# A deformable attention's depthwise taps: products on ScalarE and row sums on VectorE in place of multiply-adds on VectorE, small ScalarE work dealt out in smaller portions, three loads issued later

## The chip, the cores and the metric

The kernel runs on one core of a Trainium2 chip. The metric is device time in microseconds, the median of three runs: 3592.72 us before the change (3592.03 to 3593.57). A profiled execution, from which all views below come, had a span of 3587.1 us and a mean granted TensorE clock of 0.995.

## The reference, cut to what matters

Four layers follow one another on an image of 2 x 512 x 32 x 32. The change lies in the first, a deformable attention with 8 groups of 64 channels. Only this part matters here:

```python
q = _gconv1x1(xn, qw)                                  # per group: 64 channels, 32 x 32
qg = q.reshape(b * GROUPS, DH, H, W)
off = conv_general_dilated(qg, off_dw_w, (4, 4), ((1, 1), (1, 1)),
                           feature_group_count=DH)     # 6 x 6 taps, stride 4: 8 x 8 out
off = gelu(off + off_dw_b, approximate=False)
off = tanh(einsum('bchw,oc->bohw', off, off_pw_w)) * OFF_SCALE
...                                                    # the 64 sampling points, k and v from them
bias = sign(pos) * log1p(abs(pos))                     # 1024 pixels x 64 points x 2
bias = relu(bias @ cpb_w1 + cpb_b1)                    # to 128
bias = relu(bias @ cpb_w2 + cpb_b2)                    # 128 to 128
bias = (bias @ cpb_w3 + cpb_b3)                        # to 1
attn = softmax(einsum('bhid,bhjd->bhij', qh, kh) + bias)
out = einsum('bhij,bhjd->bhid', attn, vh)
```

The bias network runs for every pixel and every sampling point of every group. It is by far the most work of the layer; the taps, the sampling and the softmax are small beside it.

## The kernel before

Two groups make a pair; there are eight pairs `t` (two images, four each), and one loop of 256 steps (32 for each pair) runs through the bias network of all of them. A step handles four rows of points. `first` adds the two scaled tables on VectorE (line 487), into a ring of twelve buffers; `second` multiplies by `cpb_w2` on TensorE (line 504, into one of three PSUM tiles with the tag "z") and ScalarE evicts with Relu (line 512); `joined` adds two evicted parts on VectorE (line 517); a GpSimd transfer accumulates two of those; `third` (line 527) contracts with the last weights.

```python
for i in range(steps + 2):
    ...
    if i % 4 == 0 and i // 4 + 1 in tabs_of:
        scale_tabs(i // 4 + 1)
    for k, part in enumerate((1, 0, 3, 2)):
        p = 4 * i + AHEAD + k
        if p < 4 * steps:
            h1s[p] = first(p)
        if i < steps:
            parts.setdefault(i, {})[part] = second([h1s[4 * i + point] for point in range(4)], part)
        if k == 1 and i - 1 in parts:
            other = joined(parts.pop(i - 1), 2)
            if i < steps:
                nc.gpsimd.dma_start(out=joins[i - 1], in_=other, accum_op=ALU.add)
            ...
        if k % 2:
            next(behind, None)                 # one portion of the small work
        if k == 3 and i < steps:
            joins[i] = joined(parts[i], 0)
    ...
    if i >= 5 and i % 4 == 1:
        t, r = divmod(i - 5, NR)
        ...
        third(sim, r, [joins.pop(i - 5 + j) for j in range(4)])
        if r == NR - 4:
            assert next(behind, None) is None
            scores(t, sim)
            behind = chain(finish(t, sim),
                           offsets(t + 2) if t + 2 < NT else iter(()),
                           samples(t + 1) if t + 1 < NT else iter(()))
```

All that belongs to a pair beside the bias network is in generators, from which the loop takes one portion (up to the next `yield`) after every second of the four parts of a step, so two per step. Instructions of an engine keep the order of the program. `offsets` has the taps:

```python
def offsets(t):
    qpad = one.tile([P, 36, 36], F32, name="qpad", tag="pixels")
    ...                                        # q on TensorE, into qpad by ScalarE; two yields
    qv = qpad.rearrange("p (a i) (c k) -> p a i c k", i=4, k=4)
    acc = one.tile([P, HD, WD], F32, name="acc")
    for tap in range(36):
        ky, kx = divmod(tap, 6)
        src = qv[:, ky // 4 : ky // 4 + HD, ky % 4, kx // 4 : kx // 4 + WD, kx % 4]
        w = col("dw_w", tap)
        if tap == 0:
            nc.vector.tensor_scalar(acc, src, w, None, ALU.mult)              # line 331
        else:
            nc.vector.scalar_tensor_tensor(acc, src, w, acc, ALU.mult, ALU.add)  # line 333
        if tap == 33:
            table(AF.Gelu)
        if tap % 3 != 1:
            yield
    accf = acc.rearrange("p y x -> p (y x)")
    act = actbd[t % 2]
    for h in range(2):
        r = slice(h * DH, (h + 1) * DH)
        nc.scalar.activation(act[r, r], accf[r], AF.Gelu, bias=col("dw_b")[r])   # line 342
    yield
    ...                                        # tanh, positions, their logarithms, out to memory
```

`table` is a small activation that brings the function's table onto ScalarE ahead of its use. The softmax of a pair is in `finish`, the tables of the loop in `load_tabs` and `scale_tabs`:

```python
for g in range(16):                            # line 564
    nc.scalar.activation(atv[:, g, :], ptv[:, g, :], AF.Exp, bias=mx[:, g : g + 1],
                         accum_out=sm[:, g : g + 1])
    if g % 4 == 3:
        yield
nc.vector.reciprocal(sm, sm)

def scale_tabs(c):                             # two tables of 128 x 512 for every fourth step
    tx, ty = tabs_of[c]
    if c == 0:
        ...                                    # the same on VectorE
    else:
        nc.scalar.activation(tx, tx, AF.Identity, bias=col("cpb_b1"), scale=col("cpb_w1", 0))  # 473
        nc.scalar.mul(ty, ty, col("cpb_w1", 1))                                                # 474
```

Ahead of the loop, weights of a later layer are folded on TensorE (`fold`), and the order of the loads there is:

```python
def late_loads():
    load_groups("vw")
    nc.sync.dma_start(out=xs[1], in_=...)      # the second image
    nc.sync.dma_start(out=ow, in_=...)         # output weights
...
load_tabs(0)
scale_tabs(0)
late_loads()
for _ in range(3):
    advance(small_steps)
    advance(fold_steps)
drain(fold_steps)
...
for p in range(AHEAD):
    h1s[p] = first(p)                          # first(0) issues load_tabs(1)
```

Of the kernel before, what the change touches and what calls it, by code (L numbers as in the profile page):

```python
# [11 lines left out]
F32 = mybir.dt.float32  # L12
AF = mybir.ActivationFunctionType
# [66 lines left out]
def kernel(ctx: ExitStack, tc: tile.TileContext, a: dict, out: bass.AP):  # L80
# [56 lines left out]
    def layer0(l0, fold_d, t2_b, o2_b):  # L137
# [166 lines left out]
        def table(function):  # L304
            nc.scalar.activation(trial[:, 1:2], trial[:, 0:1], function)
# [4 lines left out]
        def offsets(t):  # L310
            b, pr = divmod(t, NPAIR)
            qpad = one.tile([P, 36, 36], F32, name="qpad", tag="pixels")
            nc.gpsimd.memset(qpad, 0.0)
            pq = zt([P, HW], "pq")
            for half in range(2):
                n = slice(half * HALF, (half + 1) * HALF)
                nc.tensor.matmul(pq[:, n], qws[:, pr, :], xs[b][:, pr, n], start=True, stop=True)
            yield
            nc.scalar.activation(
                qpad[:, 1:33, 1:33], pq.rearrange("p (y x) -> p y x", x=W), AF.Identity, bias=qb[:, pr : pr + 1]  # L320
            )
            yield

            qv = qpad.rearrange("p (a i) (c k) -> p a i c k", i=4, k=4)
            acc = one.tile([P, HD, WD], F32, name="acc")
            for tap in range(36):
                ky, kx = divmod(tap, 6)
                src = qv[:, ky // 4 : ky // 4 + HD, ky % 4, kx // 4 : kx // 4 + WD, kx % 4]
                w = col("dw_w", tap)
                if tap == 0:  # L330
                    nc.vector.tensor_scalar(acc, src, w, None, ALU.mult)
                else:
                    nc.vector.scalar_tensor_tensor(acc, src, w, acc, ALU.mult, ALU.add)
                if tap == 33:
                    table(AF.Gelu)
                if tap % 3 != 1:
                    yield
            accf = acc.rearrange("p y x -> p (y x)")
            act = actbd[t % 2]
            for h in range(2):  # L340
                r = slice(h * DH, (h + 1) * DH)
                nc.scalar.activation(act[r, r], accf[r], AF.Gelu, bias=col("dw_b")[r])
            yield
            po = zt([P, 2], "po")
            nc.tensor.matmul(po, act, col("pw_w", 0, 2), start=True, stop=True)
            th = two.tile([P, 2], F32, name="th")
            nc.scalar.activation(th, po, AF.Tanh)
            yield

            nxy = two.tile([P, 2], F32, name="nxy")  # L350
            nc.vector.scalar_tensor_tensor(nxy, th, 4.0, cs("gxy"), ALU.mult, ALU.add)
            nc.vector.tensor_scalar(nxy, nxy, 2.0 / 7.0, -1.0, ALU.mult, ALU.add)

            pos = two.tile([P, 2, 32], F32, name="pos")
            nc.vector.tensor_tensor(
                pos,
                cs("gq").unsqueeze(1).to_broadcast([P, 2, 32]),
                nxy.unsqueeze(2).to_broadcast([P, 2, 32]),
                ALU.subtract,
            )  # L360
            gp = two.tile([P, 2], F32, name="gp")
            nc.vector.tensor_scalar(gp, nxy, 1.0, W / 2.0, ALU.add, ALU.mult)
            nc.vector.tensor_scalar(gp, gp, -0.5, None, ALU.add)
            gps[t] = gp
            table(AF.Ln)
            yield
            sgn = two.tile([P, 2, 32], F32, name="sgn")
            nc.scalar.activation(sgn, pos, AF.Sign)
            nc.scalar.activation(pos, pos, AF.Abs)
            nc.scalar.activation(pos, pos, AF.Ln, bias=1.0)  # L370
            yield
            nc.vector.tensor_mul(pos, pos, sgn)
            nc.sync.dma_start(out=slog_d[t].rearrange("x p i -> p x i"), in_=pos)
            tables.add(t)
# [12 lines left out]
        def samples(t):  # L387
# [23 lines left out]
            wx = one.tile([P, P], F32, name="wx")  # L411
            nc.scalar.activation(wx, gpb[:, 0, :], AF.Abs, bias=cs("px"))
            nc.scalar.activation(wx, wx, AF.Relu, bias=1.0, scale=-1.0)
            wy = one.tile([P, 8, P], F32, name="wy")
            for k in range(8):
                nc.scalar.activation(wy[:, k, :], gpb[:, 1, :], AF.Abs, bias=cs("py", k))
                if k % 3 == 1:
# [46 lines left out]
                nc.sync.dma_start(out=tab, in_=src[:, rc * RCH : (rc + 1) * RCH, :].partition_broadcast(P))  # L464
                tabs_of[c].append(tab)

        def scale_tabs(c):
            tx, ty = tabs_of[c]
            if c == 0:
                nc.vector.tensor_scalar(tx, tx, col("cpb_w1", 0), col("cpb_b1"), ALU.mult, ALU.add)  # L470
                nc.vector.tensor_scalar(ty, ty, col("cpb_w1", 1), None, ALU.mult)
            else:
                nc.scalar.activation(tx, tx, AF.Identity, bias=col("cpb_b1"), scale=col("cpb_w1", 0))
                nc.scalar.mul(ty, ty, col("cpb_w1", 1))

        def first(p):

# [65 lines left out]
        def finish(t, sim):  # L543

            b, pr = divmod(t, NPAIR)
            if pr == 0:
                oTs[b] = one.tile([P, NPAIR, HW], F32, name="oT")
            oT = oTs[b]
            simb = two.tile([P, HW], F32, name="simb", tag="simb")
            nc.scalar.activation(simb, sim, AF.Identity, bias=simbias[t])  # L550
            yield
            table(AF.Exp)
            pt = zt([P, 8, P], "pt")
            for i in range(8):
                nc.tensor.transpose(pt[:, i, :], simb[:, i * P : (i + 1) * P], ident)
            ptv = pt.rearrange("p i (g j) -> p (i g) j", j=NJ)
            mx = two.tile([P, 16], F32, name="mx")
            nc.vector.tensor_reduce(mx, ptv, AX.X, ALU.max, negate=True)
            yield
            at = two.tile([P, 8, P], F32, name="at", tag="simb")  # L560
            atv = at.rearrange("p i (g j) -> p (i g) j", j=NJ)
            sm = two.tile([P, 16], F32, name="sm")
            for g in range(16):
                nc.scalar.activation(
                    atv[:, g, :], ptv[:, g, :], AF.Exp, bias=mx[:, g : g + 1], accum_out=sm[:, g : g + 1]
                )
                if g % 4 == 3:
                    yield
            nc.vector.reciprocal(sm, sm)
            nc.vector.tensor_tensor(atv, atv, sm.unsqueeze(2).to_broadcast([P, 16, NJ]), ALU.mult)  # L570
            yield
            last = t == NT - 1
            pps = []
            if last:

                pps = [zt([P, HW], "pp") for _ in range(2)]
                for m in range(2):
                    project_out(pps[m], m, range(NPAIR - 1 - m), oT)
            pa = zt([P, 8, P], "pa")
            for i in range(8):  # L580
                nc.tensor.transpose(pa[:, i, :], at[:, i, :], ident)
            if last:
                project_out(pps[1], 1, [NPAIR - 2], oT)
            aT = two.tile([P, HW], F32, name="aT", tag="simb")
            nc.scalar.copy(aT, pa.rearrange("p i j -> p (i j)"))
            yield
            pv = (ps_s if last else ps_z).tile([P, HW], F32, name="pv", tag="sim" if last else "z")
            for half in range(2):
                n = slice(half * HALF, (half + 1) * HALF)
                nc.tensor.matmul(pv[:, n], vbd[t], aT[:, n], start=True, stop=True)  # L590
                if last:
                    nc.scalar.copy(oT[:, pr, n], pv[:, n])
            if not last:
                nc.scalar.copy(oT[:, pr, :], pv)
            yield
            if pr < NPAIR - 1:
                return
            for m in range(CC):
                if m < len(pps):
                    pp = pps[m]  # L600
                    project_out(pp, m, [NPAIR - 1], oT)
                else:
                    pp = zt([P, HW], "pp")
                    project_out(pp, m, range(NPAIR), oT)
                nc.vector.scalar_tensor_tensor(xs[b][:, m, :], pp, col("out_b", m), xs[b][:, m, :], ALU.add, ALU.add)
                yield
# [103 lines left out]
        drain(steps)  # L710
        advance(small_steps, 2)
        load_tabs(0)
        scale_tabs(0)
        late_loads()
        for _ in range(3):
            advance(small_steps)
            advance(fold_steps)
# [11 lines left out]

        for p in range(AHEAD):  # L730
            h1s[p] = first(p)
        for i in range(steps + 2):
            if i == steps:
                (w1s,) = load_w(wa, "wa", [a["mlp_w1"]])
            if i % 4 == 0 and i // 4 + 1 in tabs_of:
                scale_tabs(i // 4 + 1)
            for k, part in enumerate((1, 0, 3, 2)):
                p = 4 * i + AHEAD + k
                if p < 4 * steps:
                    h1s[p] = first(p)  # L740
# [886 lines left out]
```

## Time and profile before

| what | value |
|---|---|
| median of three runs | 3592.72 us |
| loop of the first layer, from the first z to the last projection | 56.45 to 2138.5 us |
| one pair of the loop, from 836.28 to 1088.55 us | 252.27 us |
| in it: TensorE, VectorE, ScalarE busy | 249.18, 237.45, 170.21 us |
| z eviction on ScalarE (line 512, 128x1024) | 1.115 us, x1024 |
| sum of the tables on VectorE (line 487, 128x1024) | 1.22 us, x1024 |
| join on VectorE (line 517, 128x1024) | 1.28 us, x512 |
| scaling of a chunk's tables on ScalarE (lines 473 and 474) | 0.81 and 0.71 us, x63 each |

The profile gives, for one execution, the busy time of each engine, groups of instructions with their mean duration and the idle time ahead of them, a list of who waited for whom, and the chain of work that ended last: followed back from the last instruction, at each step to what released it or to the instruction before it on its engine. In the chain a line is start, duration, engine, tile and line of the program; "issue" is time in which nothing in the profile was waited for. A busy TensorE is not TensorE at its peak: a matmul of the z kind lasts 595 ns from start to end, but several run at once, so its pace has to be read from stretches of the chain. Idle time of an engine costs nothing where another one sets the pace.

### The profile page before, as it was taken

What the parts mean: (1) busy time and instruction counts of PE and PEld (TensorE: products, weight loads), DVE (VectorE), ACT (ScalarE), POOL (GpSimd) and SP (SyncE); (2) the same over time, 40 slices, a digit from 0 to 9 for tenths busy, and PEclk for the clock granted to TensorE, in tenths of its full rate; (3) what the DMA queues carried; (4) which work ended last, traced back from release to release, by engine and by line L of the source; (5) the groups of instructions that cost most, each with busy time, mean ns of one, the idle gap of its engine ahead of it and who ended that gap; (6) DMA issues with size and microseconds to landing.
All of it is one profiled execution on the core that took longest, in us unless ns stands there. A gap on an engine that the chain in (4) does not pass through costs nothing.

```text
span 3587.1 us, 57945 instructions
## 1 busy us (share of the span) xinstructions
PE 3529.7 (98%) x24777; PEld 1468.8 (41%) x24777; DVE 2507.3 (70%) x2930; ACT 1691.6 (47%) x2226; POOL 278.7 (8%) x326
## 2 busy tenths in 40 slices
PE   8999999999999999999999989999999999999999
PEld 4333333333333333233233339999633333444443
DVE  6999998998996998999998944554256365130223
ACT  3666666666664676667666631211244133111111
POOL 0111111111110111111111100000001000000000
PEclk9999999999999999999999999999999999999999
DMA  5454444454452444444444440000200000000000
GB/s 163 84 99 84 82 94 85 83 95 79 83 95 58 83 95 83 93 85 77 95 83 89 85 120 11 10 13 13 80 1 1 1 1 1 15 0 0 6 30 25
DMA packets 135963, 213.44 MB, mean 60 GB/s; under 512 B 14993, under 2 KB 93201, under 8 KB 134929
## 3 DMA queue, kind: packets, MB, share of 16 engines
q0 software_dynamic: 36720, 133.71, 19.8%
q1 hardware_dynamic: 98832, 75.41, 8.5%
q8 instruction: 197, 3.23, 0.4%
q14 instruction: 70, 0.57, 0.0%
q10 hardware_dynamic: 144, 0.52, 0.0%
HBM read 64.12 MB, written 10.75 MB: 21 GB/s over the span
## 4 chain that ended last, share of the span: by engine, by line
PE 80%; DVE 16%; issue 2%; ACT 2%; DMA 1%; SPq 0%; POOL 0%; POOLq 0%; DVEq 0%; ACTq 0%
PE z L504 33%; PE pw L135 6%; DVE wa L487 5%; PE pm L1226 5%; PE pma L135 5%; PE pmv L135 5%; DVE h L517 5%; PE pmb L135 4%; PE score L1337 4%; PE score L135 3%; PE pv L1385 3%; DVE h L487 3%; PE sim L527 2%; PE ppr L1257 2%; PE pmp L135 2%
## 5 line engine op out<-in xcount | busy, mean ns | idle before, releaser
L512 ACT ACTIVATE h<-z,b2h 128x1024 f32<-128x1024 f32 x1024 | 1134.5, 1115 | 662.9 <-PE z L504 635.8
L504 PE MATMUL z<-wa,cpb_w 128*32 128x512 f32 x10880 | 1202.0, 595 | 13.0 <-ACT h L512 13.0
L487 DVE CUSTOM_DVE_ANT_1 wa<-tab,tab 128x1024 f32<-128x1024 f32 x680 | 800.3, 1219 | 13.5 <-PE z L504 13.5
L504 PEld LDWEIGHTS z<-wa,cpb_w 128*32 128x32 f32 x10880 | 349.4, 110 | 824.5 <-issue 733.3
L517 DVE SCALAR_TENSOR_TENSOR h<-h,turn,h 128x1024 f32<-128x1024 f32 x512 | 655.0, 1279 | 21.9 <-ACT h L512 21.7
L504 PE MATMUL z<-h,cpb_w 128*32 128x512 f32 x5504 | 616.1, 597 | 14.2 <-ACT h L512 14.2
L487 DVE CUSTOM_DVE_ANT_1 h<-tab,tab 128x1024 f32<-128x1024 f32 x344 | 405.0, 1220 | 11.0 <-PE z L504 10.9
L746 POOL DMA_DIRECT2D h<-h x255 | 220.1, 863 | 1831.8 <-DVE h L517 806.3
L504 PEld LDWEIGHTS z<-h,cpb_w 128*32 128x32 f32 x5504 | 177.0, 110 | 426.9 <-issue 376.1
L1338 ACT ACTIVATE p<-score 128x1024 f32<-128x1024 f32 x144 | 139.5, 1021 | 184.8 <-PE score L1337 184.8
L135 PE MATMUL pw<-p,vT 128*128 128x512 f32 x512 | 221.8, 593 | 1.3 <-DVE y L1443 1.3
L1268 DVE TENSOR_TENSOR acc<-acc,p 128x2048 f32<-128x2048 f32 x56 | 128.8, 2301 | 105.1 <-ACT p L1338 57.8
L1121 ACT COPY p<-pma 128x128 f32<-128x128 f32 x70 | 18.6, 266 | 304.0 <-PE pma L135 304.0
L1270 DVE TENSOR_TENSOR acc<-p 128x2048 f32<-128x2048 f32 x12 | 27.5, 2291 | 183.6 <-ACT p L1472 110.0
L135 PEld LDWEIGHTS pw<-p,vT 128*128 128x128 f32 x512 | 97.0, 190 | 122.6 <-issue 121.0
L1113 DVE TENSOR_TENSOR upper<-pma,p 128x256 f32<-128x256 f32 x70 | 29.6, 423 | 163.4 <-ACT p L1121 163.3
L527 PE MATMUL sim<-h,w 128*32 128x512 f32 x1024 | 125.7, 599 | 6.6 <-DMA h<-h 6.6
L1337 PE MATMUL score<-q,k 64*128 64x512 f32 x512 | 127.2, 615 | 0.0
L1226 PE MATMUL pm<-hc,wa 128*64 128x512 f32 x512 | 122.4, 603 | 0.0
L1385 PE MATMUL pv<-p,vT 128*64 128x512 f32 x512 | 121.4, 595 | 0.0
L135 PE MATMUL score<-t,hc 128*128 128x512 f32 x256 | 110.2, 592 | 0.0
L1443 DVE TENSOR_TENSOR y<-pw,r 128x512 f32<-128x512 f32 x32 | 21.8, 682 | 115.8 <-PE pw L135 115.8
(299 smaller groups left out, 3057.8 us busy)
## 6 DMA issues: line engine op xcount, KB each, us to landing
h<-h POOLq DMA_DIRECT2D x255, 512.0 KB, 4.9
tab<-slog_d SPq DMA_DIRECT2D x128, 256.0 KB, 6.8
wa<-in_qkv_w SPq DMA_DIRECT2D x8, 768.0 KB, 6.3
xt<-in_xt SPq DMA_DIRECT2D x8, 512.0 KB, 4.9
wa<-in_mlp_w SPq DMA_DIRECT2D x4, 1024.0 KB, 10.1
wb<-in_mlp_w SPq DMA_DIRECT2D x16, 256.0 KB, 5.4
x_d<-x SPq DMA_DIRECT2D x32, 128.0 KB, 1.8
out<-x SPq DMA_DIRECT2D x16, 256.0 KB, 2.0
```

The costliest lines, as they stand in the source:

```text
L135: nc.tensor.matmul(pm, w, m, start=(k == 0), stop=(k == len(pairs) - 1))
L487: nc.vector._custom_dve(TENSOR_ADD_SAT, out=h1.rearrange("p (y x) -> p y x", x=W), in0=tx[:, quad, point, :].unsqueeze(1).to_broadcast([P, ...
L504: nc.tensor.matmul(z[point * 32 : point * 32 + 32, n], cpb_w2[:, lo : lo + 32], h1s[point][:, n], start=True, stop=True,)
L512: nc.scalar.activation(h2, z, AF.Relu, bias=b2h[:, part : part + 1])
L517: nc.vector.scalar_tensor_tensor(h2, h2, turn[:, part // 2 : part // 2 + 1], parts.pop(part + 1), ALU.mult, ALU.add)
L527: nc.tensor.matmul(sim[quad * 32 : quad * 32 + 32, n], w3[:, 28 - r : 60 - r], h2[:, n], start=(r == 0), stop=False,)
L746: nc.gpsimd.dma_start(out=joins[i - 1], in_=other, accum_op=ALU.add)
L1226: nc.tensor.matmul(pm[at : at + wide], w[:, k, lo + at : lo + at + wide], h[k][:, n], start=(k == 0), stop=(k == CC - 1),)
L1268: nc.vector.tensor_add(acc, acc, p)
L1337: nc.tensor.matmul(sc[:, part, :], ks[part][r, left[part]], qs[part][r, n], start=True, stop=True)
L1338: nc.scalar.activation(p[:, :, n], sc, AF.Exp, scale=scale)
L1385: nc.tensor.matmul(pv[part * 64 : part * 64 + 64, n], vT[:, ls, lo : lo + 64], lp[:, part, n], start=(ls == 0), stop=(ls == 7),)
```

## The change: what it does and what it is for

For the pairs 1 to 7, whose taps run inside the loop, each of the 36 taps becomes a product on ScalarE into a slot of its own, and after each row of six VectorE sums the row, with the sum so far as a seventh addend. The portions become three products each, so 12 where there were 24. VectorE has less to do in a loop that it nearly fills; ScalarE has room. Pair 0, ahead of the loop, keeps its multiply-adds. The table for Gelu is called after the taps, in a portion of its own. The 16 exponentials of a softmax are dealt out in threes, with a portion more before the reciprocal. The two scalings of a chunk's tables come one step later, one ahead of each half of that step. The loads of the value weights, the second image and the output weights are issued after the eight first sums of the loop, and so behind the load of the second chunk's tables. The buffer of the products is shared with one that the sampling uses.

```diff
             qv = qpad.rearrange("p (a i) (c k) -> p a i c k", i=4, k=4)
-            acc = one.tile([P, HD, WD], F32, name="acc")
+            accf = one.tile([P, NJ], F32, name="acc")
+            acc = accf.rearrange("p (y x) -> p y x", x=WD)
+            products = None if t == 0 else one.tile([P, 2, 7, HD, WD], F32, name="products", tag="wy")
             for tap in range(36):
                 ...
-                if tap == 0:
+                if t:
+                    nc.scalar.mul(products[:, ky % 2, kx], src, w)
+                    if kx % 3 == 2:
+                        yield
+                    if kx == 5:
+                        n = 7 if ky else 6
+                        summed = products[:, 1 - ky % 2, 6] if ky < 5 else acc
+                        nc.vector.tensor_reduce(
+                            summed.rearrange("p y x -> p (y x)"),
+                            products[:, ky % 2, :n].rearrange("p k y x -> p (y x) k"),
+                            AX.X,
+                            ALU.add,
+                        )
+                elif tap == 0:
                     nc.vector.tensor_scalar(acc, src, w, None, ALU.mult)
                 else:
                     nc.vector.scalar_tensor_tensor(acc, src, w, acc, ALU.mult, ALU.add)
-                if tap == 33:
-                    table(AF.Gelu)
-                if tap % 3 != 1:
+                if t == 0 and tap % 3 != 1:
                     yield
-            accf = acc.rearrange("p y x -> p (y x)")
+            table(AF.Gelu)
+            if t:
+                yield
 ...
-            wy = one.tile([P, 8, P], F32, name="wy")
+            wy = one.tile([P, 8, P], F32, name="wy", tag="wy")
 ...
-        def scale_tabs(c):
-            tx, ty = tabs_of[c]
+        def scale_tab(c, ax):
+            tab, w = tabs_of[c][ax], col("cpb_w1", ax)
             if c == 0:
                 ...
             else:
-                nc.scalar.activation(tx, tx, AF.Identity, bias=col("cpb_b1"), scale=col("cpb_w1", 0))
-                nc.scalar.mul(ty, ty, col("cpb_w1", 1))
+                nc.scalar.activation(tab, tab, AF.Identity, bias=0.0 if ax else col("cpb_b1"), scale=w)
 ...
-                if g % 4 == 3:
+                if g % 3 == 2:
                     yield
+            yield
             nc.vector.reciprocal(sm, sm)
 ...
         load_tabs(0)
-        scale_tabs(0)
-        late_loads()
+        for ax in range(2):
+            scale_tab(0, ax)
 ...
         for p in range(AHEAD):
             h1s[p] = first(p)
+        late_loads()
         for i in range(steps + 2):
             if i == steps:
                 (w1s,) = load_w(wa, "wa", [a["mlp_w1"]])
-            if i % 4 == 0 and i // 4 + 1 in tabs_of:
-                scale_tabs(i // 4 + 1)
             for k, part in enumerate((1, 0, 3, 2)):
+                if i % 4 == 1 and k % 2 == 0 and i // 4 + 1 in tabs_of:
+                    scale_tab(i // 4 + 1, k // 2)
                 p = 4 * i + AHEAD + k
```

More of the change, by code (lines that the diff above doesn't have):

```diff
@@ L465, in load_tabs @@
                 tabs_of[c].append(tab)
-        def scale_tabs(c):
-            tx, ty = tabs_of[c]
+        def scale_tab(c, ax):
+            tab, w = tabs_of[c][ax], col("cpb_w1", ax)
             if c == 0:
-                nc.vector.tensor_scalar(tx, tx, col("cpb_w1", 0), col("cpb_b1"), ALU.mult, ALU.add)
-                nc.vector.tensor_scalar(ty, ty, col("cpb_w1", 1), None, ALU.mult)
-            else:
-                nc.scalar.activation(tx, tx, AF.Identity, bias=col("cpb_b1"), scale=col("cpb_w1", 0))
-                nc.scalar.mul(ty, ty, col("cpb_w1", 1))
+                nc.vector.tensor_scalar(tab, tab, w, 0.0 if ax else col("cpb_b1"), ALU.mult, ALU.add)
+            else:
+                nc.scalar.activation(tab, tab, AF.Identity, bias=0.0 if ax else col("cpb_b1"), scale=w)
         def first(p):
```

## The prediction

> **What bounds the kernel now.** I read the page first. Part 1 has TensorE busy almost throughout, so I looked for where its queue was really held up.
>
> ```profile
> PE 3529.7 (98%) x24777; PEld 1468.8 (41%) x24777; DVE 2507.3 (70%) x2930; ACT 1691.6 (47%) x2226; POOL 278.7 (8%) x326
> L333 DVE SCALAR_TENSOR_TENSOR acc<-qpad,pc,acc 128x64 f32<-128x64 f32 x280 | 92.4, 330 | 4.2
> ```
>
> The change concerns the attention of the first layer, which runs to about 2138 us. There VectorE spends 92.4 us on the taps: 36 per pair of groups (line 333 x35 plus one opening product), 36 x 0.33 = 12 us. The chain of work that ended last gives TensorE's pace where nothing disturbs it:
>
> ```profile
> 1049.42 27.47 PE z L504 x256
> ```
>
> 27.47 / 256 = 0.1073 us per matmul instruction. A step of the loop holds 64 of them (6.87 us), and every fourth step adds 16 of line 527 (1.72 us): 7.30 us per step on average. VectorE needs in a step 4 sums of 1.22 us and 2 joins of 1.28 us, 7.44 us. So the two are within 2% of each other, and the ring of twelve buffers lets one lead the other for a while. The chain of one pair, from 836.28 to 1088.55 (a period of 252.27 us; four other pairs repeat it within 0.2 us), shows which of them costs time:
>
> ```profile
> 843.40 0.02 issue
> 843.42 0.06 ACT h L512
> 843.48 0.96 issue
> 844.44 1.28 ACT at L564 x8
> 845.73 0.70 ACT tab L473
> 846.43 0.61 ACT tab L474
> 847.04 1.01 ACT h L512
> ...
> 878.14 0.29 DVE acc L331
> ...
> 969.37 0.03 ACT actbd L342
> 969.39 0.34 issue
> 969.73 0.34 ACT actbd L342
> 970.07 0.03 issue
> 970.10 0.81 ACT tab L473
> 970.91 0.61 ACT tab L474
> 971.52 1.01 ACT h L512
> 972.53 0.04 issue
> 972.58 12.20 PE z L504 x96
> ```
>
> From 878 to 969 the chain runs over VectorE, sums, joins and taps in turn. That looks like the bound, but is not the loss. Between 875.92 and 972.58 (96.66 us) TensorE executed 833 z and 48 sim instructions and two small ones, 94.8 us at its own pace: it lost 1.9 us, and all of that at the end. The waits of TensorE in the pair agree:
>
> ```profile
> PE z L504 <- ACT h L512: 3.1, 2, 1.9
> ```
>
> Two stalls, both behind ScalarE's eviction of z: 1.2 us at 848, where four exponentials and both scalings of a table (1.28 + 1.52 us) stand ahead of it; and 1.9 us at 972, where ScalarE waits for the last tap, does two Gelus, and then again both scalings. After the second, 96 instructions take 12.20 us and not 10.3: another 1.9.
>
> At the top, the timeline from 56 us on:
>
> ```profile
> 64.61 0.81 ACT L473 ACTIVATE tab<-tab,pc 128x512 f32<-128x512 f32 x1 [7.04 <-DMA tab<-slog_d]
> 68.74 5.25 PE L504 MATMUL z<-h,cpb_w 128*32 128x512 f32 x32 [6.74 <-ACT h L512]
> ```
>
> The first step asks ScalarE to scale the second chunk's tables before it evicts anything. They land 7 to 8 us after their issue at 57.96, so TensorE stands for 6.74 us, then runs slowly (5.25 us where 3.43 is its pace).
>
> [...] the granted clock is 0.81 between 968.6 and 975.9, and weight loads come every 0.86 us there instead of 0.43. A stall of 1.9 us thus costs about 3.8, while the 1.2 us one at 848 is not followed by slow matmuls. [...] the trace has 324 ns for the 128x64 exponentials of line 564. [...] No row of the kernel before reduces with a stride of 256 bytes, so no run here shows it yet.
>
> **The change, part by part.**
>
> Taps, for pairs 1 to 7: VectorE loses 12 us per pair and gets six reductions, one of 384 and five of 448 elements. From 686 ns for 512 and 1212 for 1024 (line 1274) the slope is 1.03 ns and the start about 0.16 us, so 0.55 to 0.62 us each, 3.7 us per pair: 8.3 us per pair less. If the stride doubles the price per element, they are 0.95 to 1.08 us, 6.4 us per pair, still a saving of 5.6. [...] z has three buffers in PSUM, and an eviction may be late by about 1.7 us more than with two, so I expect these products to delay TensorE hardly at all.
>
> None of the 8.3 us is TensorE's time by itself. What counts is that the Gelu no longer waits for VectorE with ScalarE's queue behind it: the reduction is queued half a step before, the table load and the Gelu get a slot each, and the taps take 12 slots of the loop where they took 24, so the Gelu does not meet the scalings. I take off the whole stall and the slow matmuls after it: 1.9 + 1.9 = 3.8 us per pair.
>
> Attention: groups of three exponentials (0.96 us) instead of four, and the two scalings apart, one before each half of a later step. The worst accumulation becomes about 0.96 + 0.81 = 1.8 us instead of 2.8. The present 1.28 us groups without scalings cause no stall and 2.8 causes 1.2, so about 1.5 is free and 1.8 costs 0.3: 0.9 us less per pair. The scores' PSUM tile is held one step longer; I add 0.4 us per pair for that and for products and scalings that meet.
>
> So each of the five alike pairs gives 3.8 + 0.9 - 0.4 = 4.3 us, together 21.5. A second count checks this: z 2048 and sim 128 instructions at 0.1073 (233.5 us) plus the small matmuls of a pair (pk 2.2, pq, pv and scores 1.9 each, pt and pa 1.0 each, gpb and pkv 0.6 each, pb and po 0.3 each: 11.8) are 245.3 us, and about 2 us of small steps between kinds of matmul stay: 247.3. A period of 248 lies just above it. The pair with the output projection (1088.55 to 1365.89) has only the first stall: 0.7. The last stretch has two waits of 1.2 each (2.4 in all), both with scalings in them: 1.8.
>
> Top: with the scaling moved to the second step, ScalarE is free when z starts at 56.45, and the tables that landed at 64.6 and 67.0 are asked for at about 65 and 68.5. The three loads now queue behind these tables instead of ahead of them, and none is used before about 217 us (the value weights). That removes 6.7 + 1.8 us. The stretch to 331.94 has also a 1.4 us stall at 188, where samples and scalings meet, of which I take 1.3. Together 9.8.
>
> Sum: 21.5 + 0.7 + 1.8 + 9.8 = 33.8 us; 3592.7 - 33.8 = 3559.
>
> **The rivals.** (1) TensorE takes it all: VectorE leaves the chain but TensorE had lost nothing to it, and only the top and the attention improve, 9.8 + 8 x 0.8 = 16 us, 3576. For it speaks that TensorE never waits for a tap in the trace; against it, the 1.9 us wait at 972 starts with ScalarE waiting 1.2 us for line 333. (2) ScalarE becomes the bound: with products in front of the evictions of 12 half steps per pair, and 0.3 us lost in each, 7 x 12 x 0.3 = 25 us go back, 3584. For it: both stalls of today are ScalarE's. Against it: with three buffers there are some 3 us of slack[...]. (3) The strided reductions are several times dearer: at 3 us each VectorE would need 18 us per pair instead of 12 and hold up the sums, and the kernel would be slower, about 3600. [...] (4) The later loads collide with the accumulating transfers of the first steps: their first user comes some 30 us later, so at most 2 us.
>
> **Range and chances.** The gain is a sum of small stalls, each seen in the trace; I could be wrong by half of the pairs' part (11 us) or by a third of the top (3 us). 3549 to 3570. A gain of over 2% would need 72 us, more than all idle time that TensorE has in this stage (2082 us less its own 2046 of busy time is 36, plus clock losses): 0.01. Slower by 2% would need rival 3 at its worst: 0.01.
>
> **What would show it.** Right: a period near 248 us for the alike pairs; no wait of TensorE over 1 us in them and no z piece of 12.2 us for 96 instructions; no wait at 61 to 68; reductions of 0.6 us, products of 0.3; VectorE's busy time down by about 58 us, ScalarE's up by about 70 (its durations overlap). Wrong: the same 252 with z waiting for ScalarE behind `products`, or reductions well over 1.1 us with TensorE waiting for VectorE's sums, or the first eviction still waiting for a table.

## The result, and the profile after

The changed kernel takes 3559.06 us (median, 3554.58 to 3559.85) against 3593.09 us for the kernel before, whose runs were repeated beside it: a ratio of 0.9903, with a 95% interval of 0.9886 to 0.992. That is 34.0 us or 1% less, and the predicted 3559.

The page of the changed kernel, its line of engines, and from the list of groups the products, the row sums and the scalings:

```profile
PE 3522.7 (99%) x24777; PEld 1469.1 (41%) x24777; DVE 2479.0 (70%) x2720; ACT 1760.6 (50%) x2478; POOL 278.1 (8%) x326
L335 ACT ACTIVATE products<-qpad,pc 128x64 f32<-128x64 f32 x252 | 85.5, 407 | 0.0
L341 DVE TENSOR_REDUCE products<-products 128x64 f32<-128x448 f32 (+1 forms) x35 | 33.5, 956 | 2.6 <-ACT products L335 2.6
L489 ACT ACTIVATE tab<-tab,pc 128x512 f32<-128x512 f32 x126 | 96.3, 764 | 0.0
```

ScalarE has 69 us more to do and VectorE only 28 us less: the products are 407 ns where 0.3 us was expected, the row sums 956 ns where 0.6 us was. TensorE's busy time went down by 7 us, with the same instructions.

One of the five alike pairs, of the same kind as the one shown before (there 252.27 us), lies from 573.91 to 821.46 us and lasts 247.55 us. Its waits of TensorE, and the chain, first at the only place where it leaves TensorE and then around the Gelu:

```profile
PE z L519 <- ACT h L527: 0.5, 1, 0.5
```

```profile
573.91 13.99 PE z L519 x128
587.90 0.02 issue
587.92 0.04 ACT h L527
587.97 0.97 issue
588.94 0.99 ACT at L579 x6
589.93 0.70 ACT tab L489
590.63 1.01 ACT h L527
591.64 0.04 issue
591.69 3.64 PE z L519 x32
...
660.67 13.73 PE z L519 x128
674.41 0.31 PE po L362 x2
674.72 10.44 PE z L519 x96
```

The stretch of 90 us that ran over VectorE in the chain is gone. What the Gelu releases (`po`, line 362) starts while z runs, and the 96 instructions after it take 10.44 us instead of 12.20. Where four exponentials (x8 in the chain, each with the reading of its sum) met both scalings, three now meet one, and TensorE waits 0.5 us instead of 1.2.

The difference of the two profiled spans (3587.1 and 3556.6) can be laid out completely, by the start of the first z and by the starts of `pt`, the transposes that end each pair:

| stretch | before, us | after, us | difference | predicted |
|---|---|---|---|---|
| start to the first z | 56.45 | 61.94 | +5.5 | 0 |
| first z to the first `pt` | 274.4 | 263.3 | -11.1 | -9.8 |
| five alike pairs | 1261.2 | 1237.8 | -23.4 | -21.5 |
| pair with the output projection | 277.35 | 277.01 | -0.3 | -0.7 |
| last pair | 236.95 | 235.50 | -1.5 | -1.8 |
| all that follows | 1480.8 | 1481.1 | +0.3 | 0 |
| sum | 3587.1 | 3556.6 | -30.5 | -33.8 |

So the pairs gave 2 us more than predicted and the top 4 us less, because the first z starts 5.5 us later. The timed medians differ by 3.5 us more than the profiles do, mostly because the execution of the kernel before that was profiled took 3588.89 us, 4.2 less than the median. The windows around 31 to 43 us show why z starts later. In them the columns are window, length, busy time of TensorE, weight loads, VectorE, ScalarE, GpSimd, the granted clock (1.00 is full speed), then two of the transfers. The changed kernel:

```profile
28.00:31.00 3.00, 2.42 (x14) 1.51 (x12) 2.68 (x9) 1.55 (x4) 1.18 (x1) 1.00 0.00 0
31.00:34.00 3.00, 2.53 (x14) 2.53 (x14) 1.95 (x14) 2.45 (x7) 0.00 (x0) 0.64 0.42 175
34.00:37.00 3.00, 3.00 (x15) 3.00 (x16) 2.60 (x5) 0.27 (x2) 0.00 (x0) 0.50 0.07 11
37.00:40.00 3.00, 3.00 (x4) 1.22 (x4) 2.75 (x5) 0.00 (x0) 0.00 (x0) 0.50 0.38 74
40.00:43.00 3.00, 3.00 (x7) 1.20 (x5) 0.55 (x1) 0.00 (x0) 0.00 (x0) 0.65 0.64 73
```

The kernel before, at the same place in its program:

```profile
34.00:37.00 3.00, 3.00 (x9) 1.33 (x9) 2.93 (x6) 0.00 (x0) 0.00 (x0) 1.00 0.10 16
37.00:40.00 3.00, 3.00 (x14) 1.82 (x13) 2.25 (x4) 0.00 (x0) 0.00 (x0) 1.00 0.82 69
```

The program of TensorE is the same there. The clock fell to half for some ten microseconds in one execution and not in the other. That the change causes this is not shown: further down, the kernel before with only its loads moved had the clock at half for 6.9 us there, and the changed kernel with the rows side by side for only 3.4.

### The profile page after: what moved, and what is told of

It is laid out like the page before. It is cut to its first block, busy times and chain, and to the rows that moved or that the text cites. A ratio compares the mean times of both kernels' runs of the same rounds, so it can differ in the third digit from the quotient of the medians.

```text
span 3556.6 us, 58202 instructions
## 1 busy us (share of the span) xinstructions
PE 3522.7 (99%) x24777; PEld 1469.1 (41%) x24777; DVE 2479.0 (70%) x2720; ACT 1760.6 (50%) x2478; POOL 278.1 (8%) x326
## 4 chain that ended last, share of the span: by engine, by line
PE 96%; DVE 1%; ACT 1%; issue 1%; DMA 0%; POOL 0%; POOLq 0%; DVEq 0%; ACTq 0%
PE z L519 49%; PE pw L135 6%; PE pm L1243 5%; PE pma L135 5%; PE pmv L135 5%; PE pmb L135 4%; PE score L1354 4%; PE sim L542 3%; PE score L135 3%; PE pv L1402 3%; PE ppr L1274 2%; PE pmp L135 2%; PE pp L628 2%; PE pf L135 1%; PE pma L1216 1%
## 5 line engine op out<-in xcount | busy, mean ns | idle before, releaser
L519 PE MATMUL z<-h,cpb_w 128*32 128x512 f32 x5504 | 608.7, 593 | 0.9 <-ACT h L527 0.9
```

Source lines behind the costliest of these rows:

```text
L519: nc.tensor.matmul(z[point * 32 : point * 32 + 32, n], cpb_w2[:, lo : lo + 32], h1s[point][:, n], start=True, stop=True,)
```

## The experiments

**Theories.** A: the time was lost in ScalarE's queue. The two scalings of a table (1.5 us), set into the loop every fourth step, met other small work of ScalarE in front of an eviction: the exponentials, the Gelu, the first eviction of all. What matters is which portion of small work falls beside the scalings. B: the time was lost to VectorE's load of 12 us of taps per pair, which made it late, and with it the Gelu. The change touches both at once.

### The products alone

The kernel before with the products, the row sums and the Gelu's own portion; exponentials, scalings and loads as they were.

```diff
+                if t:
+                    nc.scalar.mul(products[:, ky % 2, kx], src, w)
+                    ...                        # row sums on VectorE, 12 portions
+            table(AF.Gelu)
+            if t:
+                yield
```

> The kernel before with the products on ScalarE and the Gelu in its own portion, all else as before. Theory A (a pair's 4.7 us came from collisions in ScalarE's queue: the Gelu no longer stands in line with two scalings, and the softmax's groups no longer with both): the stall at the Gelu and the slow matmuls after it go, the 1.2 us at the exponentials and the wait at the top stay: a pair of about 248.5 us, and five alike pairs give 19 us: about 3573. Theory B (VectorE's relief by 6 us a pair is what counts): the same here within 2 us. The top wait of 6.7 us stays in both.

Measured: 3575.23 us, ratio 0.9966 (0.9955 to 0.9978) against its own runs of before; a pair 248.9 us. The wait at the top stays (7.1 us), and the exponentials still meet both scalings, 1.2 us. So the products and the Gelu's own portion, taken alone, give 3.4 of the 4.7 us per pair. Both theories had expected this, so it does not tell them apart. The absolute time is as expected; the ratio gives 12 us rather than 19, since the pair with the output projection became 2.3 us longer (279.7 us) and before itself ran between 3587 and 3596 us on that chip.

### The scalings alone

The kernel before, with only the two scalings moved and parted.

```diff
 ...                                           # scale_tabs becomes scale_tab, as in the change
-            if i % 4 == 0 and i // 4 + 1 in tabs_of:
-                scale_tabs(i // 4 + 1)
             for k, part in enumerate((1, 0, 3, 2)):
+                if i % 4 == 1 and k % 2 == 0 and i // 4 + 1 in tabs_of:
+                    scale_tab(i // 4 + 1, k // 2)
```

> The kernel before with only the two scalings of a chunk one step later and apart; taps on VectorE, fours of exponentials and loads as before. Theory A: nothing stands behind the Gelu or among the exponentials any more, and the first eviction waits for no table: a pair of about 248 us, top 8 us shorter (or 3, if the array's clock drops at 31 us as it did in the changed kernel): 3560 to 3566. Theory B: VectorE still does 12 us of taps a pair and holds the Gelu up, so only the exponentials (1.2 us a pair) and the top gain: about 3577.

Measured: 3563.04 us, ratio 0.9925 (0.9908 to 0.9942); a pair 248.35 us. B falls: VectorE still does every tap, and the chain of this pair still runs over it for 90 us, but all of the loss save 0.8 us is gone. The end of that stretch, from the chain of the pair at 575.67:

```profile
708.53 0.35 DVE acc L333
708.87 0.02 issue
708.90 0.03 ACT actbd L342
708.92 0.34 issue
709.26 0.35 ACT actbd L342
709.61 0.02 issue
709.63 1.12 ACT h L510
710.75 0.04 issue
710.79 10.51 PE z L502 x96
```

The Gelu waits for the last tap as before, but one eviction follows it directly, without scalings in between, and the 96 instructions after it take 10.51 us. Of the 4.7 us per pair, the scalings' place alone gives 3.9. This and the 3.4 of the products alone are not to be added, since both take the Gelu away from the scalings. The wait at the top is gone as well: the list of waits has no entry over 0.6 us before z.

### All but the products

The changed kernel with the taps on VectorE again, in 24 portions; the rest of the change kept.

```diff
-                if t:
-                    nc.scalar.mul(products[:, ky % 2, kx], src, w)
-                    ...
+                if tap == 0:
+                    nc.vector.tensor_scalar(acc, src, w, None, ALU.mult)
+                else:
+                    nc.vector.scalar_tensor_tensor(acc, src, w, acc, ALU.mult, ALU.add)
+                if tap % 3 != 1:
+                    yield
```

> The changed kernel with the taps back on VectorE in 24 portions of one or two, and everything else of the change kept, the Gelu's table in its own portion too. Theory A: the move of the taps is not needed: a pair within 1 us of 247.55, the kernel within 7 us of the changed one, 3559 to 3566. Theory B: VectorE's 8.4 us per step against TensorE's 7.3 for twelve steps comes back as lost time: a pair of about 251 us, about 3578.

Measured: 3561.09 us, ratio 0.9925 (0.9908 to 0.9941); a pair 248.22 us. With all the rest of the change in place, the products, which name it, are worth 0.66 us per pair. In the chain of this pair the sampling's activations meet a scaling, which they do not in the changed kernel, where the taps take 12 portions fewer and the sampling comes earlier:

```profile
740.96 0.88 ACT wy L417 x3
741.84 0.70 ACT tab L473
742.54 1.01 ACT h L511
```

TensorE waits 0.4 us for this. So a good half of what remains of the products' worth, too, is seen in the trace as a place in the queue; the rest, 0.3 us, I can't place.

### The loads alone

```diff
         scale_tabs(0)
-        late_loads()
 ...
             h1s[p] = first(p)
+        late_loads()
         for i in range(steps + 2):
```

> The kernel before with only the three loads issued after the eight first sums. If the late issue of those loads is what freed the top: the first eviction's wait of 6.7 us shrinks to 3 us or less, 3587 to 3589. If it was the scaling's later place (theory A): the second chunk's tables are still issued at 58 us behind the last folded weights and land 7 to 9 us later, the wait stays at 6 to 7 us, and the time is within 2 us of 3593.

Measured: 3589.14 us, ratio 0.9998 (0.999 to 1.0007): nothing. The second table of the second chunk is on the way for 10.8 us, and TensorE's longest wait is 9.0 us where it was 6.7. It was the scaling's later place that freed the top.

A side finding: four of the five alike pairs of this trace take 250.5 us and not 252.3, though their program is that of the kernel before. The stall at the Gelu is there in all five (1.9 to 2.0 us, in one 1.15), but slow matmuls follow it in one only. TensorE behind the Gelu in the pair at 588.74, and then in the one at 1617.73, which takes 252.2 us:

```profile
726.09 3.64 PE L504 MATMUL z<-h,cpb_w 128*32 128x512 f32 x32 [1.92 <-ACT h L512]
```

```profile
1755.08 5.33 PE L504 MATMUL z<-wa,cpb_w 128*32 128x512 f32 x32 [1.92 <-ACT h L512]
```

The same wait of 1.92 us is followed by 32 matmuls in 3.64 us and in 5.33. So the slow matmuls do not follow from the length of the stall, and 1.7 of the 4.7 us by which the pairs differ lay in the profiled execution of the kernel before and need not lie in another.

### The Gelu half a step later

The kernel before with one `yield` more; no engine gets less work.

```diff
             accf = acc.rearrange("p y x -> p (y x)")
+            if t:
+                yield
             act = actbd[t % 2]
```

> The kernel before with one thing added: a yield between the last tap and the Gelu of pairs 1 to 7, so that the Gelu comes half a step later and stands behind the two scalings instead of ahead of them. No engine gets less work. Theory A (collision in ScalarE's queue): the 1.9 us stall and the slow matmuls after it go; the sampling's activations shift by half a step too and now meet the next scalings, which may cost about 1 us: a pair of 248.5 to 250, the kernel 10 to 19 us faster than before. Theory B (VectorE's load): a pair of 252.3, the same time.

Measured: 3584.18 us, ratio 0.9987 (0.9979 to 0.9996); a pair 250.6 us. That is less than expected (the period lies 0.6 us above the range and the gain is some 5 us), but the two effects are those named. The period is also no shorter than the 250.5 us that an unchanged pair takes where no slow matmuls follow the stall; what this run shows is the moved stall, not a gain per pair. The profiled execution, at 3589.06 us, was one of the longer ones. From the chain of the pair at 586.99:

```profile
704.94 20.60 PE z L506 x192
725.54 0.31 PE po L347 x2
725.86 7.06 PE z L506 x64
...
750.94 0.88 ACT wy L418 x3
751.82 0.70 ACT tab L475
752.51 0.61 ACT tab L476
753.12 1.01 ACT h L514
```

The stall at the Gelu is gone by a change of place alone, and a new one of 1.1 us stands where three of the sampling's activations now meet both scalings. About 1 us per pair of the shortfall I can't place.

### Exponentials in fours

```diff
-                if g % 3 == 2:
+                if g % 4 == 3:
                     yield
-            yield
             nc.vector.reciprocal(sm, sm)
```

> The changed kernel with the exponentials dealt out in fours again and without the additional portion. Theory A (only exponentials that meet a scaling hurt): the last group now comes before both scalings, so the pair is 247.1 to 247.6 and the kernel 3556 to 3559. My prediction's view that groups of three are worth something: the pair becomes 248 or more, the kernel 3562 or more.

Measured: 3561.67 us, ratio 0.992 (0.9904 to 0.9937); a pair 248.33 us. My expectation was wrong, the prediction's sign right: threes and the added portion together are worth 0.78 us per pair. But the exponentials themselves cause no wait here. From the chain and the waits of the pair at 570.7:

```profile
682.57 0.19 ACT near L423
682.76 0.71 ACT tab L489
683.47 1.01 ACT h L527
```

```profile
PE z L519 <- ACT h L527: 0.7, 1, 0.7
PE pa L596 <- DVE at L585: 0.2, 1, 0.2
```

With two portions fewer in the softmax everything behind it moves up by a whole step, and now the sampling's first activations meet a scaling; besides, the transposes wait for VectorE's normalisation, which lost its portion of distance.

### A row's addends side by side

```diff
-one.tile([P, 2, 7, HD, WD], F32, name="products", tag="wy")
+one.tile([P, 2, HD, WD, 7], F32, name="products", tag="wy")
...
-                            products[:, ky % 2, :n].rearrange("p k y x -> p (y x) k"),
+                            products[:, ky % 2, :, :, :n],
```

> The changed kernel with the seven addends of an output side by side in memory, so that VectorE reads each sum contiguously and ScalarE writes with a stride of 28 bytes. If the stride of 256 bytes is what makes a reduction 975 ns and not the 620 of my estimate: 600 to 650 ns, and the products slower or equal. If it is a cost of short sums or of tensor_reduce itself: still 900 to 1000. In either case TensorE bounds the loop: the pair stays within 0.3 us of 247.55 and the kernel within 2 us of the changed one.

Measured: 3556.54 us, ratio 0.9908 (0.9892 to 0.9925); a pair 247.55 us, unchanged. The instructions on the tile of products, shortest, median and longest in ns, in this kernel and then in the changed one:

```profile
L335 ACT ACTIVATE products<-qpad,pc x252: 398/410/449, 72.0 to 1681.4; 128x64 f32<-128x64 f32 x126
L341 DVE TENSOR_REDUCE products<-products x35: 546/616/625, 77.5 to 1675.1; 128x64 f32<-128x448 f32 x28, 128x64 f32<-128x384 f32 x7
```

```profile
L335 ACT ACTIVATE products<-qpad,pc x252: 393/405/449, 76.0 to 1685.5; 128x64 f32<-128x64 f32 x126
L341 DVE TENSOR_REDUCE products<-products x35: 859/974/997, 81.5 to 1680.2; 128x64 f32<-128x448 f32 x28, 128x64 f32<-128x384 f32 x7
```

Reading with a stride of 256 bytes costs 0.36 us in a sum of 448, 0.8 ns per element; writing with a stride of 28 bytes costs ScalarE next to nothing (a median of 410 against 405 ns). VectorE gets 2 us per pair back, and not a tenth of a microsecond of it reaches the pair.

### A dense fold at the thin place

The changed kernel, with the order at the top changed so that one group of fold matmuls runs while the first pair's offset is on its way.

```diff
         advance(fold_steps, 2)
         drain(bias_steps)
+        advance(steps)
+        advance(fold_steps)
         drain(steps)
 ...                                           # one group less in the loop of three that follows
```

> The changed kernel with one group of the dense fold matmuls set between the reordering of the weights and the first pair's offset product, where TensorE stood for 1 us and then did single columns. If the halved clock from 31 to 42 us comes from that thin stretch: it goes, z starts at 56 to 57.5 us and not at 62, and the kernel takes about 3554.5, as the fastest run of the changed kernel did. If the drop has another cause, z still starts at 61 to 62 and the time stays at 3559.

Measured: 3553.3 us, ratio 0.9896 (0.988 to 0.9913). z starts at 57.5 us. The clock no longer falls at 31 us, but it falls from 38.6 to 42.2, behind 24 single-column matmuls that now stand in a row. One start of z proves little: with the rows side by side, where the top is that of the changed kernel, z started at 57.9 in the profiled execution, and with fours at 59.1. What speaks for the place is the times, 3552.7 to 3556.6 us in four runs against 3554.6 to 3559.9, and the cure is incomplete.

### Both ends

The same, and the last but one join added on VectorE, so that no transfer is waited for at the end of the loop.

```diff
-                    if i < steps:
+                    if i < steps - 1:
                         nc.gpsimd.dma_start(out=joins[i - 1], in_=other, accum_op=ALU.add)
```

> The fold moved ahead as in e5_fold_ahead, and the last join but one of the loop added on VectorE instead of by a transfer, for which TensorE waits 5.8 us at the end. If both ends are as I read them: 4.5 us at the top and 3 to 5 at the end, 3550 to 3552 against 3559 for the changed kernel. If only the end: 3555.

Measured: 3549.11 us, ratio 0.9885 (0.9868 to 0.9901), runs from 3548.7 to 3549.2, a microsecond below the expected range. The waits of TensorE at that place, in the changed kernel and then in this one:

```profile
PE sim L542 <- DMA h<-h: 5.8, 1, 5.8
```

```profile
PE sim L542 <- DVE h L768: 3.0, 1, 3.0
```

The last pair became 5.1 us shorter (230.4 against 235.5). The wait accounts for 2.8 of it; the rest is slow matmuls, which follow the wait in the changed kernel (12 of line 542 take 3.63 us) and not here (10 take 1.90).

### All of it, with the single columns dealt out

As above, the addends side by side, and the single-column products set between the folds.

```diff
         drain(bias_steps)
+        advance(steps)
+        advance(small_steps)
+        advance(fold_steps)
         drain(steps)
-        advance(small_steps, 2)
         load_tabs(0)
+        advance(small_steps)
         for ax in range(2):
             scale_tab(0, ax)
+        advance(fold_steps)
         for _ in range(3):
```

> Both ends as in e8_both_ends, with the single-column products at the top dealt out among the dense folds so that they never come 24 in a row, and the addends of a row side by side as in e6_rows_together. If the remaining clock drop at 37 to 43 us (about 1.7 us) goes: 3547 to 3548. If it stays: 3549, as e8_both_ends; the side-by-side rows are expected to bring nothing, as TensorE bounds the pairs.

Measured: 3548.86 us, ratio 0.9882 (0.9866 to 0.9899). The clock stays at 1.00 from 28 to 52 us in the profiled execution and z starts at 55.4, two microseconds earlier than with both ends alone; the last pair took 1.5 us longer (231.9 against 230.4), so the time is the same within half a microsecond. Behind the same wait of 2.96 us the 10 matmuls of line 542 took 3.43 us here and 1.90 there. These two kernels are the quickest of the study, 10 us below the changed one.

## Why the prediction was right, point by point

The total came out right, and most of its terms did. That it met 3559 within 0.1 us is luck. Between the two profiled executions the gain is 30.5 us and not 33.8: the pairs gave 2 us more than predicted and the top 4 less. The medians differ by 34 because the kernel before took 4 us more in its median than in the profiled execution. In the runs repeated beside the experiments its medians were 3588.2 to 3591.1, and the changed kernel's four runs spread over 5 us.

**What bounds the kernel.** Right. The prediction read 245.3 us of TensorE's own work from the trace and 247.3 with the steps between kinds of matmul; the pair now takes 247.55 with one wait of 0.5 left. The reading that the long stretch of the chain over VectorE was not where the time went is shown by the kernel with the scalings alone, which keeps that stretch and loses 0.8 us. One sum was off: VectorE's 7.44 us per step adds durations from start to end, and these overlap where the instructions follow each other. From the chain of the kernel before:

```profile
895.18 2.27 DVE h L487 x2
897.45 1.20 DVE h L517
```

Four sums and two joins in a row are so 6.9 us, below TensorE's 7.30 and not above it; only the taps brought VectorE over it for twelve steps.

**Taps: 3.8 us per alike pair.** The size was right, the share open. I took the stall at the Gelu off because the sum is queued earlier, because the Gelu has a portion of its own, after that of its table's load (1.28 us), and because it no longer meets the scalings. Two ways of getting there were tried apart: moving the scalings alone takes the pair from 252.3 to 248.35 us, the products and the portion alone to 248.9. Either suffices, and the second adds little to the first: with scalings, threes and loads in place, the products add 0.66 us. That VectorE's relief is not needed is shown by the scalings alone, where it still does every tap.

**Row sums and products.** The row sums were taken as 0.55 to 0.62 us, with 0.95 to 1.08 if the stride doubled the price per element: they are 0.87 and 0.98, so the price rose by some three quarters. That this is the stride is shown by the sums of adjacent addends, whose median is 0.616 us. The products were expected at 0.3 us, near the 0.324 of the exponentials of line 564 on as many elements, and are 0.405. VectorE's busy time was to fall by 58 us and fell by 28, in part because the row sums are longer and in part because the taps had overlapped with their neighbours (the durations, added up, fell by 40). ScalarE's was to rise by 70, an estimate of mine that no run had shown, and rose by 69. None of it mattered, as TensorE bounds the pair in every variant.

**Attention: 0.9 off, 0.4 on.** 0.5 us are left of the 1.2, where I had left 0.3; of the 0.4 added for new meetings no wait is seen. The free allowance behind an eviction, taken as about 1.5 us, comes out at 1.2 (0.99 + 0.70 us of small work, 0.5 of wait). That the threes as such are better is not shown: in fours, away from both scalings, they cause no wait either, and what changed with them was which later portion meets a scaling.

**Slow matmuls after the Gelu: 1.9.** Gone, as predicted; but the price was wrong as a rule. I had taken it that a stall of 1.9 us costs 3.8. The loads-alone kernel has stalls of 1.9 to 2.0 us at the same place in four pairs, and slow matmuls behind one of them. What decides it is not shown.

**Top: 9.8.** The stretch from the first z on gained 11.1. The step that failed is the silent assumption that z starts where it did: it started 5.5 us later, with TensorE's clock at 0.50 ahead of it. Of the 11.1, the scaling's later place alone gives 9.0; with the taps back on VectorE 2.5 are missing, so the products seem to be worth the rest; the later loads alone do nothing.

**Rivals.** The first, that only the top and the attention improve (16 us), falls with the pair at 247.55. The second, ScalarE as the bound, falls: behind the 36 products of an alike pair no wait of TensorE is seen. The 1.7 us for a third buffer of z and the slack of some 3 us were estimates, from 16 matmuls at 0.107 us to a buffer; a slack of that size is not seen, as 1.69 us of small work already leaves a wait of 0.5. The third, sums of 3 us, falls with 0.97. The fourth, loads that collide with the first transfers, costs nothing: the second table of the second chunk lands 10.9 us after its issue and not 8.5, but before it is asked for, and TensorE has no wait from 62 to 326 us.

## What to carry to other kernels

Where small work is dealt out in portions beside a loop that one engine fills, ask of each portion what else stands in the same queue at that moment (in the kernel before, the first eviction of z stood behind both scalings, one of which had waited 7.04 us for its table); a fixed insertion every few steps and a generator of small portions beat against each other. Here moving the insertion by one step was worth 3.9 us per pair, and moving the taps to another engine, which also changed the portions, 3.4 alone but only 0.7 on top of it. A long stretch of the chain over another engine is not yet a loss: count the bound engine's own instructions in that stretch and compare. Two changes that each remove the same stall must be tried both alone and on top of each other. And look at the whole queue after each shift, since a portion moved away from one collision may move another into one.

## What the runs showed of the hardware that I had not expected

- The clock of TensorE fell to 0.50 between 31 and 43 us in ten of the twelve profiled executions, for about 3.4, 6.8 or 10.3 us (the changed kernel from 31.6 to 42.0). There is no long gap ahead of it: in the changed kernel TensorE does ten short matmuls, stands for 1 us, and then does two of two columns, eight of 128, among which the clock falls, and 16 of one column. The mean clock differs from run to run of one kernel (the changed kernel's run of 3554.58 us had 0.998, its others, at 3559 to 3560, 0.996 to 0.997). What decides when it falls is not shown. The kernel before and the one that deals the single columns out had 1.00 in this stretch, each in one profiled execution.
- A stall of 1.92 us was followed by 1.7 us of slow matmuls in one pair and by none in another of the same trace.
- A strided read costs VectorE's sum 0.8 ns per element more (974 against 616 ns), and a strided write costs ScalarE's 64-element product 5 ns in all (410 against 405).
- Three products in a row take ScalarE 1.0 us. With three PSUM buffers for z, TensorE waited for none of the twelve such portions in an alike pair.
